# A query-bias product for four pairs at once: stationary and moving sides exchanged in a cross-attention kernel

## The chip, the core and the metric

The kernel runs on one core of a Trainium2 chip. The metric is the device time of one execution in microseconds (us), the median over several runs. The engines are TensorE (PE in the profile, with its weight loads as PEld), VectorE (DVE), ScalarE (ACT), GpSimd (POOL) and SyncE (SP, which here only issues DMAs). SBUF is the core's working memory, PSUM the memory with eight banks that TensorE writes to.

## The reference, cut to what matters

The program is one block of a Perceiver: cross-attention of 64 queries over 1601 context rows, for a batch of 8; then an attention among the 64 queries with 16 heads; then a layer of eight experts of which each token takes one. All is float32. The change touches the cross-attention alone:

```python
qp = layernorm(x) @ Wq + bq            # (8, 64, 512)
kp = ctx @ Wk + bk                     # (8, 1601, 512)
vp = ctx @ Wv + bv
attn = softmax((qp @ kp.T) / sqrt(512))
x = x + attn @ vp
```

The kernel never forms kp. It uses qp·kp = (qp·Wkᵀ)·ctx + qp·bk. The second term is one number per query, called q.bk or `qb` here. It is added to every score of its row.

## The kernel before

The 8 x 64 = 512 tokens are handled as four pairs of batch entries, 128 tokens each (`NT` = 4, `P` = 128). Channels (512) are four chunks of 128 (`DC` = 4). The helper names below are those of the code.

**The start.** x is normalised with tokens on partitions and transposed on TensorE (`turn_x`, L271), so that channels lie on partitions (`xnT`). `project_q` (L279) multiplies by Wq and writes `qpT`: query channels on partitions, tokens along the free side. It runs once for pair 0 (L298) and once for pairs 1 to 3 together (L835). ScalarE adds bq while it copies from PSUM (L289).

**Two products of each pair's queries.** `keyed(p)` (L308) computes qp·Wkᵀ, with tokens on partitions; ScalarE copies it to a row `qk` (L313). `biased(p)` (L315) computes q.bk: the pair's queries are the stationary side, a 128x128 block for each of four chunks, and one column of `bk` is the moving side. The result, one column with tokens on partitions, is copied by ScalarE to column p of `qb` (L324). The softmax needs it in that form: one number per partition, read by VectorE in L375 and L377.

**The scores.** `spread(p)` (L326, GpSimd) repeats each run of 32 channels of qk four times, and `fill_queries` (L345) transposes these on TensorE into the tile `R` (L349; ScalarE copies at L352). The context comes by DMA with rows on partitions. VectorE turns it into blocks of 32 by 32 (`blocks`, L245, with L233 and L240), four of whose parts make a tile `T`; five buffers (pool `blk`) hold the T tiles, and the softmax's `L` tiles too. `scores` (L354) multiplies T by R for a quarter of the channels, in tiles of 32 rows by 64 columns of the array, into four PSUM banks. `softmax` (L367) follows on VectorE and ScalarE, `chances` (L400) transposes the result, and `attend` (L409) multiplies by the context.

**Order.** TensorE's order is written out by hand from L252 on (a manual schedule); that of ScalarE is too in the block at L829. Elsewhere the tile framework orders each engine's instructions by its own planning, from their place in the program and their dependencies. So a line moved in the program moves exactly on TensorE, and about so on VectorE and ScalarE.

**The loop.** From L851, for each pair p, four quarters of scores with earlier stages of pair p-2 among them, the softmax, then preparation of the next pair, then `attend` in four groups. In pair 0 the preparation has `keyed` and `biased` for pairs 1 to 3 one after the other (L879 to L883), then `tables` (L629), whose product is `gs` (L639).

**Buffers.** Big tiles (weights, context, `xnT`, `qpT`) are slabs, of which there are 12. The loads of pair 1's context and of the next weights wait in SP's queue until a slab comes free: the one of `wkT` after the last `keyed`, that of `qpT` after its last reader, those of the context after `attend`. PSUM tiles take whole banks, eight in all.

Of the kernel before, what the change touches and what calls it, by code (L numbers as in the profile page):

```python
# [10 lines left out]
F32 = mybir.dt.float32  # L11
# [6 lines left out]
P = 128  # L18
B, S, D = 8, 64, 512
SK = 1601  # L20
NT = B * S // P
DC = D // P
# [14 lines left out]
def perceiver_kernel(ctx: ExitStack, tc: tile.TileContext, out: bass.AP, t: dict):  # L37
    nc = tc.nc
# [6 lines left out]
    rowp = pool(name="rows", bufs=22)  # L45
# [5 lines left out]
    def slab(name):  # L51
        return slabs.tile([P, DC, D], F32, tag="slab", name=name)

    def row(name):
        return rowp.tile([P, D], F32, tag="row", name=name)
# [4 lines left out]
    def bank(name):  # L60
        return banks.tile([P, D], F32, tag="bank", name=name)

    def bank4(name):
        return banks.tile([P, DC, P], F32, tag="bank", name=name)
# [25 lines left out]
    ident = const.tile([P, P], F32, tag="ident", name="ident")  # L90
    make_identity(nc, ident)

    def load_c(name, shape, queue):
        c = const.tile(shape, F32, tag=name, name=f"c_{name}")
        return c, queue.dma_start(out=c, in_=t[name])

    def load_late(name, shape):
        c, ins = load_c(name, shape, nc.gpsimd)
        tc.keep_in_program_order(ins)
        return c  # L100

    def load_b(name, n, c=None):
        if c is None:
            c = const.tile([P, n], F32, tag=name, name=f"c_{name}")
        tc.keep_in_program_order(
            nc.gpsimd.dma_start(out=c, in_=t[name].partition_broadcast(P))
        )
        return c

    bq, _ = load_c("xbq", [P, DC], nc.scalar)  # L110
    bk, _ = load_c("xbk", [P, DC], nc.scalar)
# [22 lines left out]
    qb = const.tile([P, NT], F32, tag="qb", name="qb")  # L134
# [110 lines left out]
    def blocks(p, q, b2):  # L245

        T = block_tile(p, q, b2)
        for g in range(4):
            turn_group(T, p, q, b2, g)
        return T  # L250
# [4 lines left out]
    qpT = slab("qpT")  # L255
# [15 lines left out]
    def turn_x(i, xn):  # L271
        tp = transposed(xn, f"xn{i}")
        step = 2 if i == 0 else DC
        for dc in range(0, DC, step):
            nc.scalar.copy(  # L275
                xnT[:, dc : dc + step, i * P : (i + 1) * P], tp[:, dc : dc + step, :]
            )
# [30 lines left out]
    def keyed(p):  # L308

        cols = slice(p * P, (p + 1) * P)  # L310
        ps = projected(qpT[:, :, cols], wkT, f"qk{p}")
        qks[p] = row(f"qk{p}")
        nc.scalar.copy(qks[p], ps)  # L313

    def biased(p):  # L315

        cols = slice(p * P, (p + 1) * P)
        ps = bank(f"qb{p}")
        for ec in range(DC):
            nc.tensor.matmul(  # L320
                ps[:, 0:1], lhsT=qpT[:, ec, cols],
                rhs=bk[:, ec : ec + 1], start=(ec == 0), stop=(ec == DC - 1),
            )
        nc.scalar.copy(qb[:, p : p + 1], ps[:, 0:1])  # L324

    def spread(p):  # L326

        qk = qks.pop(p)
        got = []
        for b0 in range(0, NB, 4):  # L330
            q4 = rowp.tile([P, 4, 4, 32], F32, tag="row", name=f"q4_{p}_{b0}")
            nc.gpsimd.tensor_copy(  # L332
                q4,
                qk[:, 32 * b0 : 32 * b0 + 128].rearrange(
                    "p (b d) -> p b d", d=32
                ).unsqueeze(2).to_broadcast([P, 4, 4, 32]),
            )
            got.append(q4)
        return got

    def queries(p):

        return one.tile([P, NB, P], F32, tag="R", name=f"R_{p}")

    def fill_queries(p, R, q4s, half):  # L345
        for b0 in range(8 * half, 8 * half + 8, 4):
            tp = bank4(f"rt_{p}_{b0}")
            for j in range(4):
                nc.tensor.transpose(  # L349
                    tp[:, j, :], q4s[b0 // 4][:, j, :, :].rearrange("p a d -> p (a d)"), ident  # L350
                )
            nc.scalar.copy(R[:, b0 : b0 + 4, :], tp)  # L352

    def scores(p, q, R, sc, Ts, js=range(4)):  # L354
        for j in js:
            b = 4 * q + j
            for a in range(4):
                for b2 in range(2):
                    r = b2 * S
                    nc.tensor.matmul(  # L360
                        sc[a][r : r + S, : WIDTH[a]],
                        lhsT=R[32 * a : 32 * a + 32, b, r : r + S],
                        rhs=Ts[b2][32 * a : 32 * a + 32, j, : WIDTH[a]],
                        start=(b == 0), stop=(b == NB - 1),
                    )
# [456 lines left out]
    def quarter(p, q):  # L822
        return [blocks(p, q, b2) for b2 in range(2)]

    def do(*steps):
        for f, i in steps:
            f(i)

    with tc.manual_schedule(engines={mybir.EngineType.Activation}):  # L829
        keyed(0)  # L830
        for i in range(1, NT):
            turn_x(i, later[i - 1])
        biased(0)
    q4s = spread(0)
    project_q(1, NT - 1, [bank(f"qp1_{ec}") for ec in range(DC)])  # L835
    R = queries(0)
    fill_queries(0, R, q4s, 0)
    fill_queries(0, R, q4s, 1)
    bv = load_b("xbv", D, row("c_xbv"))
    lnw = load_late("lnw", [P, DC])  # L840
    lnb = load_late("lnb", [P, DC])
# [9 lines left out]
    for p in range(NT):  # L851
        i = p - 2
        if 0 < p < NT - 1:
            q4s = spread(p + 1)
        sc = [bank(f"sc_{p}_{a}") for a in range(4)]
        for q in range(4):
            if p == 0 and q == 0:
                nTs = [first[1, 0], first[1, 1]]
            elif p == 0 and q == 1:
                nTs = [first[2, 0], blocks(0, 2, 1)]  # L860
            else:
                nTs = quarter(p, q + 1) if q < 3 else None
            if i >= 0 and q == 3:
                scores(p, q, R, sc, Ts, range(3))
                do((back, i))
                scores(p, q, R, sc, Ts, (3,))
            else:
                scores(p, q, R, sc, Ts)
            Ts = nTs
            if i >= 0 and q < 3:  # L870
                do(((split, align, sums)[q], i))
        L, r = softmax(p, sc)
        pts = []

        def chance():
            pts.append(chances(p, len(pts), L))

        if p == 0:
            for k in range(1, NT):  # L879
                keyed(k)  # L880
                biased(k)
                if k == 1:
                    q4s = spread(1)  # L883
            tables()
        else:
            do((at_turn, p - 1))
            if i >= 0:
                do((output, i))
        if p + 1 < NT:
            R = queries(p + 1)  # L890
            if p == 0:
                chance()
                fill_queries(1, R, q4s, 0)
            elif p == 1:
                fill_queries(2, R, q4s, 0)
                do((at_out, 0))
                chance()
            else:
                do((at_out, p - 1))
                fill_queries(p + 1, R, q4s, 0)  # L900
                chance()
            fill_queries(p + 1, R, q4s, 1)
        else:
            at_out(p - 1, chance)
        if 0 < p < NT - 1:
            load_pair(p + 1)
        if p == 1:
            blank_rows()
        ac = bank(f"ac_{p}")
        if i >= 0:  # L910
            do((face, i))
        for g in range(4):
            if g < 3:
                chance()
            if p > 0 and g == 3:
                do((turn, p - 1))
            attend(p, g, pts[g], ac)
            if p > 0 and g == 0:
                do((norm, p - 1))
            if i >= 0 and g == 0:  # L920
                do((gated, i))
            if i >= 0 and g == 1:
                do((routed, i))
        tile_of[p]["acs"] = divided(p, ac, r)
        if 0 < p < NT - 1:
            do((unit_q, p - 1))
            Ts = quarter(p + 1, 0)
            do((unit_k, p - 1), (gates, p - 1), (values, p - 1))
        elif p == 0:
            Ts = quarter(1, 0)  # L930
# [92 lines left out]
    ps = bank("pc")  # L1023
# [14 lines left out]
    with tc.If(spill != 0), ExitStack() as ph:  # L1038
# [4 lines left out]
        for i in range(NT):  # L1043
            x3 = row(f"dx3_{i}")
            layernorm(x3, xs[i], f"d{i}")
            tp = ps_g.tile([P, DC, P], F32, tag="gu", name=f"dxt{i}")
# [8 lines left out]
        for e in range(E):  # L1055
# [11 lines left out]
                wb, lhsT=ones, rhs=dg.rearrange("p i q -> p (i q)"), start=True, stop=True  # L1067
# [6 lines left out]
            for ic in range(IC):  # L1074
                pgu = []
                for k in range(2):
                    ps = ps_g.tile([P, B * S], F32, tag="gu", name=f"dgu{e}_{ic}_{k}")
                    for dc in range(DC):
                        c0 = k * FI + ic * P
                        nc.tensor.matmul(  # L1080
                            ps, lhsT=wgu[:, dc, c0 : c0 + P], rhs=xsT[:, dc, :],
                            start=(dc == 0), stop=(dc == DC - 1),
# [6 lines left out]
            for i in range(NT):  # L1089
                for ic in range(IC):  # L1090
                    nc.tensor.matmul(
                        acc[i], lhsT=h[:, ic, i * P : (i + 1) * P], rhs=wd[:, ic, :],
                        start=(e == 0 and ic == 0), stop=(e == E - 1 and ic == IC - 1),
# [58 lines left out]
```

## Time and profile before

| What | Value |
|---|---|
| Median of 3 runs | 303.27 us (302.66 to 303.32) |
| Profiled execution, device time | 302.67 us |
| Its span, first to last instruction | 300.9 us |
| Mean granted TensorE clock | 0.995 of full |
| qb products (L320), passes and busy time | 32, 3.8 us |
| qb copies (L324) | 4, 0.159 us median |
| Mean DMA rate over the span | 192 GB/s |

The profile is of one execution. Its rows group instructions by line, engine, operation and the program's names, with the shape of the tile written and read. A float32 product appears as two passes, so four products of one `biased` are eight matmul rows. A matmul's end is modelled, and successive ones overlap in the records: for the cost of a group take the distance from its start to the start of the next, not the length of its rows. The waits name the engine, what it waited for, the total, the number of times and the longest. A share of busy time is an average over very different stages: the first 45 us, where data is still coming in, and the rest.

### The profile page before, as it was taken

To read this page: it belongs to the slowest core of one execution; us is meant where nothing else is said; L and a number is where in the kernel's file an instruction comes from. 1 tells how busy PE (TensorE), PEld (TensorE's weight loads), DVE (VectorE), ACT (ScalarE), POOL (GpSimd) and SP (SyncE) were. 2 spreads that over 40 slices of the span, in tenths; PEclk is the share of its full clock that TensorE was granted. 3 is DMA by queue.
4 is the path that set the end of the run, shared out by engine and by line. 5 is a ranking of instruction groups with operands and counts; after the bars stand their busy time and mean duration, and the time that the engine had idled before them with its cause. 6 is when DMAs were issued, how large, how long until landed. Compare 5 with 4: busy or idle time off the path is not lost. (4 is left out here: it accounts for less than half of the span.)

```text
span 300.9 us, 6426 instructions
## 1 busy us (share of the span) xinstructions
PE 287.7 (96%) x2652; PEld 149.0 (50%) x2652; DVE 161.7 (54%) x412; ACT 91.8 (31%) x198; POOL 61.0 (20%) x93
## 2 busy tenths in 40 slices
PE   6999899999999999999999999999999999899991
PEld 5866655743554344656434475443454557343320
DVE  2465469135743487956568785552472475364230
ACT  2223205330037021417704134632426324121110
POOL 4065200500081004200220300032050032203301
PEclk9999999999999999999999999999999999999997
DMA  6999960279984993000299102969990200603601
GB/s 187 350 417 396 345 271 1 54 296 395 397 291 151 347 418 105 3 2 0 85 408 367 51 4 67 344 190 353 370 353 4 72 0 2 210 34 94 190 2 43
DMA packets 20288, 57.71 MB, mean 192 GB/s; under 512 B 2274, under 2 KB 10514, under 8 KB 16544
## 3 DMA queue, kind: packets, MB, share of 16 engines
q1 hardware_dynamic: 17568, 50.37, 46.8%
q0 software_dynamic: 2400, 6.89, 6.2%
q8 instruction: 23, 0.38, 0.5%
q14 instruction: 9, 0.07, 0.1%
q10 hardware_dynamic: 288, 0.00, 0.1%
HBM read 50.94 MB, written 6.84 MB: 192 GB/s over the span
## 5 line engine op out<-in xcount | busy, mean ns | idle before, releaser
L233 DVE STREAM_TRANSPOSE T<-cx 128x512 f32<-128x512 f32 x96 | 61.8, 680 | 25.0 <-DMA cx<-in_ctx_dram 18.6
L360 PE MATMUL sc<-T,R 32*64 32x416 f32 (+2 forms) x1024 | 49.5, 501 | 1.5 <-DVE T L233 1.0
L416 PE MATMUL ac<-cx,pt 128*64 128x512 f32 x192 | 43.8, 598 | 0.0
L360 PEld LDWEIGHTS sc<-T,R 32*64 32x64 f32 x1024 | 26.6, 131 | 19.1 <-issue 7.1
L416 PEld LDWEIGHTS ac<-cx,pt 128*64 128x64 f32 x192 | 12.7, 136 | 22.4 <-issue 21.6
L960 PE MATMUL gu<-wgu,xeT 128*32 128x512 f32 x192 | 23.0, 597 | 0.0
L492 POOL TENSOR_TENSOR gm_k<-qn_k,c_gk 128x512 f32<-128x512 f32 x4 | 5.1, 1272 | 62.5 <-DVE qn_k L487 42.8
L455 POOL TENSOR_TENSOR x<-x,c_bo 128x512 f32<-128x512 f32 x4 | 5.1, 1268 | 59.5 <-DVE xh L454 59.5
L284 PE MATMUL qp<-xnT,w_xWq 128*128 128x128 f32 (+1 forms) x64 | 16.2, 424 | 0.5 <-ACT xnT L275 0.5
L332 POOL COPY q<-qk 128x512 f32<-128x512 f32 x16 | 9.0, 611 | 34.3 <-ACT qb L324 21.3
L185 PE MATMUL p_qk<-w_xWkT,qpT 128*128 128x512 f32 x32 | 15.0, 605 | 0.0
L185 PE MATMUL p_q<-w_aWq,xhT 128*128 128x512 f32 x32 | 14.8, 605 | 0.0
L185 PE MATMUL p_k<-w_aWk,xhT 128*128 128x512 f32 x32 | 14.7, 595 | 0.0
L185 PE MATMUL p_po<-w_xWv,acT 128*128 128x512 f32 x32 | 14.7, 595 | 0.0
L185 PE MATMUL p_o<-w_aWo,cT 128*128 128x512 f32 x32 | 14.5, 596 | 0.0
L406 ACT COPY pt<-pp 128x512 f32<-128x512 f32 (+1 forms) x16 | 8.3, 516 | 20.4 <-PE pp L404 20.2
L185 PE MATMUL p_v<-w_aWv,xvT 128*128 128x512 f32 x32 | 14.4, 592 | 0.0
L284 PEld LDWEIGHTS qp<-xnT,w_xWq 128*128 128x128 f32 x64 | 11.5, 230 | 5.0 <-ACT xnT L275 0.9
L371 DVE TENSOR_REDUCE mx<-sc 128x1 f32<-128x416 f32 (+2 forms) x16 | 8.1, 567 | 10.8 <-PE sc L360 10.8
L995 PE MATMUL y<-wd,hT 128*32 128x512 f32 x96 | 11.5, 596 | 0.6 <-DVE hT L987 0.6
L960 PEld LDWEIGHTS gu<-wgu,xeT 128*32 128x32 f32 x192 | 6.0, 109 | 8.9 <-issue 8.2
L185 PEld LDWEIGHTS p_q<-w_aWq,xhT 128*128 128x128 f32 x32 | 5.7, 189 | 9.0 <-issue 5.9
(189 smaller groups left out, 398.8 us busy)
## 6 DMA issues: line engine op xcount, KB each, us to landing
cx<-in_ctx_dram SPq DMA_DIRECT2D x24, 1024.0 KB, 9.9
wgu<-in_wgT_dram SPq DMA_DIRECT2D x8, 512.0 KB, 9.3
wgu<-in_wuT_dram SPq DMA_DIRECT2D x8, 512.0 KB, 10.0
wd<-in_wdT_dram SPq DMA_DIRECT2D x8, 512.0 KB, 9.6
rd<-blank POOLq DMA_DIRECT2D x6, 258.0 KB, 5.0
in<-rd SPq DMA_DIRECT2D x6, 258.0 KB, 4.2
xd<-blank POOLq DMA_DIRECT2D x6, 256.0 KB, 4.3
in<-xd SPq DMA_DIRECT2D x6, 256.0 KB, 7.2
```

The source lines that it names most:

```text
L185: nc.tensor.matmul(ps, lhsT=srcT[:, dc, :], rhs=w[:, dc, :], start=(dc == 0), stop=(dc == DC - 1),)
L233: nc.vector.transpose(T[:, :, 128 * g : 128 * g + 128].rearrange("p b (c k) -> p b c k", k=32), cxs[p, g][b2][:, :, 128 * q : 128 * q + 12 ...
L284: nc.tensor.matmul(ps[ec][:, : n * P], lhsT=wq[:, dc, ec * P : (ec + 1) * P], rhs=xnT[:, dc, cols], start=(dc == 0), stop=(dc == DC - 1),)
L332: nc.gpsimd.tensor_copy(q4, qk[:, 32 * b0 : 32 * b0 + 128].rearrange("p (b d) -> p b d", d=32).unsqueeze(2).to_broadcast([P, 4, 4, 32]),)
L360: nc.tensor.matmul(sc[a][r : r + S, : WIDTH[a]], lhsT=R[32 * a : 32 * a + 32, b, r : r + S], rhs=Ts[b2][32 * a : 32 * a + 32, j, : WIDTH[a ...
L371: nc.vector.tensor_reduce(mx[:, a : a + 1], sc[a][:, : WIDTH[a]], AX.X, ALU.max)
L406: nc.scalar.copy(pt[:m, :nch, :], tp[:m, :nch, :])
L416: nc.tensor.matmul(ac[r : r + S, :], lhsT=pt[:m, j, r : r + S], rhs=rhs, start=(g == 0 and j == 0), stop=(g == 3),)
L455: nc.gpsimd.tensor_tensor(xs[i], xs[i], bo, ALU.add)
L492: nc.gpsimd.tensor_tensor(heads(gm), heads(qn), gb.unsqueeze(1).to_broadcast([P, H, HD]), ALU.mult)
L960: nc.tensor.matmul(ps[c, :], lhsT=xTs[k][:, dc, c], rhs=ffw[e][0][:, dc, :], start=(dc == 0), stop=(dc == DC - 1),)
L995: nc.tensor.matmul(y[c, :], lhsT=hT[:, ic, c], rhs=ffw[e][1][:, ic, :], start=(ic == 0), stop=(ic == IC - 1),)
```

## The change

The four calls of `biased(p)` become one `biased()`. It runs after all queries are there: after the transposes that fill `R` for pair 0, before the first scores. Now `bk` is the stationary side: for each chunk, one column is read 32 times over (a broadcast), which makes a 128x32 block. The queries of a pair move, 128 tokens at a time. The four pairs write to four groups of 32 partitions of one PSUM bank, so that pair p uses the array's p-th group of 32 columns. Each of the 32 partitions of a group then holds the same row: q.bk for 128 tokens along the free side. ScalarE copies the 128x128 block to SBUF.

A new `unturned` brings tokens to partitions: one 128x128 transpose on TensorE, issued behind the first quarter of pair 0's scores, and a VectorE copy of every 32nd column from PSUM into `qb` (128x4). The readers of `qb` are unchanged.

```diff
-    def biased(p):
-
-        cols = slice(p * P, (p + 1) * P)
-        ps = bank(f"qb{p}")
+    def biased():
+
+        ps = bank("qb")
         for ec in range(DC):
-            nc.tensor.matmul(
-                ps[:, 0:1], lhsT=qpT[:, ec, cols],
-                rhs=bk[:, ec : ec + 1], start=(ec == 0), stop=(ec == DC - 1),
-            )
-        nc.scalar.copy(qb[:, p : p + 1], ps[:, 0:1])
+            for p in range(NT):
+                nc.tensor.matmul(
+                    ps[32 * p : 32 * p + 32, :P],
+                    lhsT=bk[:, ec : ec + 1].to_broadcast([P, 32]),
+                    rhs=qpT[:, ec, p * P : (p + 1) * P],
+                    start=(ec == 0), stop=(ec == DC - 1),
+                )
+        qbT = rowp.tile([P, P], F32, tag="row", name="qbT")
+        nc.scalar.copy(qbT, ps[:, :P])
+        return qbT
+
+    def unturned(qbT):
+        tp = bank4("t_qb")
+        nc.tensor.transpose(tp[:, 0, :], qbT, ident)
+        nc.vector.tensor_copy(qb, tp[:, 0, ::32])
...
             turn_x(i, later[i - 1])
-        biased(0)
     q4s = spread(0)
     project_q(1, NT - 1, [bank(f"qp1_{ec}") for ec in range(DC)])
     R = queries(0)
     fill_queries(0, R, q4s, 0)
     fill_queries(0, R, q4s, 1)
+    qbT = biased()
...
             else:
                 scores(p, q, R, sc, Ts)
             Ts = nTs
+            if p == 0 and q == 0:
+                unturned(qbT)
...
             for k in range(1, NT):
                 keyed(k)
-                biased(k)
                 if k == 1:
                     q4s = spread(1)
```

## The prediction

> **What bounds the kernel now.** I read the page first, for the engines' shares and the clock; then TensorE's waits over the whole span; then its timeline from the start to 62 us, with VectorE's and ScalarE's beside it; and last the same engines where pair 1 starts.
>
> ```profile
> span 300.9 us, 6426 instructions
> PE 287.7 (96%) x2652; PEld 149.0 (50%) x2652; DVE 161.7 (54%) x412; ACT 91.8 (31%) x198; POOL 61.0 (20%) x93
> ```
>
> TensorE is busy for 96% of the span (its ends are modelled, so this alone proves little). Its list of waits is the stronger evidence:
>
> ```profile
> PE idle L118 <- POOL ident masks.py:199: 2.0, 1, 2.0
> PE t_c L177 <- DVE cg L552: 1.6, 2, 1.1
> PE sc L360 <- DVE T L233: 1.0, 1, 1.0
> PE y L995 <- DVE hT L987: 0.6, 1, 0.6
> PE sc L360 <- DVE T L240: 0.6, 1, 0.6
> ```
>
> Between 45 and 237 us only one wait is listed, 0.3 us at 91.16. So a microsecond of TensorE work there is a microsecond of the span, if its feeders keep up. Before 45 us it does wait, and there its work is cheap. The changed products stand on both sides of that border, in TensorE's timeline:
>
> ```profile
> 17.89 0.95 PE L320 MATMUL qb<-c_xbk,qpT 128*128 128x1 f32 x8
> 18.89 10.59 PE L284 MATMUL qp<-xnT,w_xWq 128*128 128x384 f32 x32
> 29.31 1.91 PE L349 MATMUL rt<-ident,q 128*128 128x128 f32 x16
> 31.15 0.91 PE L360 MATMUL sc<-T,R 32*64 32x416 f32 x2
> 33.03 8.64 PE L360 MATMUL sc<-T,R 32*64 32x416 f32 x192 [0.97 <-DVE T L233]
> 42.24 3.02 PE L360 MATMUL sc<-T,R 32*64 32x416 f32 x62 [0.57 <-DVE T L240]
> 45.19 3.70 PE L185 MATMUL p_qk<-w_xWkT,qpT 128*128 128x512 f32 x8
> 48.72 0.95 PE L320 MATMUL qb<-c_xbk,qpT 128*128 128x1 f32 x8
> 49.53 3.68 PE L185 MATMUL p_qk<-w_xWkT,qpT 128*128 128x512 f32 x8
> 53.05 0.95 PE L320 MATMUL qb<-c_xbk,qpT 128*128 128x1 f32 x8
> 53.86 3.68 PE L185 MATMUL p_qk<-w_xWkT,qpT 128*128 128x512 f32 x8
> 57.38 0.95 PE L320 MATMUL qb<-c_xbk,qpT 128*128 128x1 f32 x8
> 58.19 0.39 PE L639 MATMUL gs<-c_gwT,ones 128*128 128x32 f32 x2
> ```
>
> Columns: start, length, engine, line, what, count. Each float32 product stands as two passes (four products, x8). The first qb fills a wait; the other three stand between products that follow without a gap. VectorE and ScalarE at the same places:
>
> ```profile
> 17.26 1.57 ACT L275 COPY xnT<-t_xn 128x512 f32<-128x512 f32 x3
> 32.27 1.30 DVE L233 STREAM_TRANSPOSE T<-cx 128x512 f32<-128x512 f32 x2 [1.28 <-DMA cx<-in_ctx_dram]
> 36.16 1.90 DVE L233 STREAM_TRANSPOSE T<-cx 128x512 f32<-128x512 f32 x3 [2.58 <-PE sc L360]
> 41.92 0.26 DVE L240 STREAM_TRANSPOSE T<-tail 96x128 f32<-96x128 f32 x1
> ```
>
> So pair 0's scores are set by VectorE: the first quarter waits until 33.03 for a tile that a DMA holds back; its end frees the buffer for three more tiles (36.16 to 42.18, no gap); the last quarter waits for these at 42.24.
>
> [...]little is saved by one column: eight passes at 128x1 take 0.81 us start to start, 0.10 each, while a 128x128 transpose takes 0.11 (8 in 0.88 at 140.46). [...]four transposes between scores take 0.59 (131.65 to 132.24) against 0.44 for four amid other transposes, 0.15 for in and out. [...]the experts' 128*32 products at 512 columns issue four in 0.43 us (weight loads at 228.01 and 228.44), which is what one 512-column pass takes alone (p_k's eight in 3.43).
>
> **The change, part by part.**
> 1. Removed behind 45 us: three qb blocks. Start to start: 49.53-48.72, 53.86-53.05 and 58.19-57.38, 0.81 each, 2.43. A p_qk behind another should also take 3.43, as p_k does (109.79 to 113.22), instead of the 3.52 seen beside qb: up to 0.18 more. I take -2.5 (-2.4 to -2.6). No cover hides these. What is late next, with TensorE 2.5 earlier: gs and the first transposes of L would run at 55.7 and 56.0; L's exponentials end at 52.4. The 16 transposes for R need GpSimd's copies of qk1, issued from 53.04 at 0.6 each, four by 55.3; they would be asked for from about 56.4. Both are in time by 1 us or more.
> 2. Removed at 17.89: the block of pair 0. The product behind it starts at 18.89, right after ScalarE's last xnT copy ends (17.26+1.57=18.83). Worth 0; TensorE waits there instead. The four tiny ScalarE copies (0.16 each) stand where ScalarE has idle time: 0.
> 3. Added behind the 16 transposes at about 31.2: 16 products, 32 passes of 128*32 by 128 columns, as eight rounds of four column groups. A round costs at least 128/512 of 0.43, 0.107; if the weight load (0.109 for 32 columns on the page) isn't hidden, 0.22. That is 0.9 to 1.8 us, with 0.2 to 0.3 for mode changes 1.1 to 2.0; I take 1.3. The queries are all there (ScalarE's L289 ends at 30.1). Behind them on TensorE stands the first score, which can't pass 33.03 anyway: 1.8 us of cover from 31.2. So 0, at worst +0.2; without the cover it would be +1.3, as it would also push the start of VectorE at 36.16. If the groups do not overlap it is much more (rival 3).
> 4. Added: a 128x128 ScalarE copy at about 32.5. ScalarE's R copies end at 32.03 and it then idles for 16.5 us: 0.
> 5. Added after the first quarter of scores (about 35.9): one transpose between scores, 0.11+0.15=0.26 on TensorE. The quarters behind it end at 41.7+0.26=41.9, still before 42.24, where the last waits for VectorE. Hidden: 0.
> 6. Added on VectorE: a copy of 128x4 from PSUM, in the very stretch (36.16 to 42.18) that ends the wait at 42.24. Nearest row: the 128x8 reduction L644, 0.19. If it stands among the tiles it costs 0.2 in full; if the compiler puts it ahead of them, VectorE waits for the transpose too (0.3 to 0.4) and it costs 0.6; behind them it is free. What waits behind it is the tiles, and for these the scores. I take +0.2 (0 to +0.6).
> 7. SP's queue: loads at 57.57 wait for the slabs of wkT and qpT, which the last p_qk now frees about 1.5 us earlier (57.4 to about 55.8), so pair 1's context starts earlier too. They move by 1.5 where TensorE moves by 2.3. Pair 1's scores start at 73.61 and VectorE's last tile before them ends at 72.55: 1.06 of slack, minus up to 0.8. Just enough: 0, at worst +0.5. Later loads are issued when TensorE's attention products free slabs, so they move with it. GpSimd's queue gets nothing.
>
> Sum: -2.5+0.2=-2.3 for the span. The profiled execution took 302.67, which gives 300.4. It is 0.6 below the median of the runs shown (303.27; the three lie at 302.66, 303.27 and 303.32), from which it would be 301.0. I say 300.7, between them.
>
> **The rivals.**
> 1. VectorE's stretch takes more back: the copy leads the tiles (0.6 instead of 0.2), and the new products outlast their cover a little (+0.2). For it: the stretch has no gap at all. Against: a tile is ready before the copy is. -2.5+0.8=-1.7: 301.3.
> 2. The gain is swallowed where pair 1 starts: its context tiles, or an order on VectorE or ScalarE that comes out otherwise, hold the scores at about 73. For it: the DMA engines are 73 to 101% busy from 58 to 74 us, and the slack is 1.06. Against: the loads themselves are released by TensorE. If 0.8 to 1.8 is lost: -1.5 to -0.5, say 301.9.
> 3. Slower: the column groups do not overlap when the stationary side is one column repeated 32 times, and each pass runs alone. Price: the 128-column passes of the first query product take 5.66/32=0.177 each; 32 make 5.7 us, from 31.2 to 36.9. Past the cover of 1.8 this delays the first quarter, then VectorE at 36.16, by 3.9. -2.3+3.9=+1.6: 304.6. It decides from about 4.1 us for the block (1.8 of cover and 2.3 of gain), 0.13 a pass. Against: the experts' products overlap; for: no row has a repeated stationary column.
> 4. The change does less than it says: the removed blocks were hidden. Only the one at 17.89 is; at the other three no wait is recorded.
>
> **How the numbers follow.** Forecast (300.7) 0.62; rival 1 0.14; rival 2 0.10; rival 3 or another late feeder of its size 0.14. A change of 0.2%, 0.6 us, is about what a measurement of this kernel can tell from none. The forecast, rival 1 and most of rival 2 are faster: 0.82; the rest of rival 2 and the edge of rival 3 are the same: 0.06; slower: 0.12. The range: from the best ends (-2.6 on the profiled execution, 300.1) down to 300.0, and up through rivals 1 and 2 to 302.4, where 0.14 is left above and little below.
>
> **What would show it.** Right: p_qk blocks of 3.43 to 3.5 us back to back, gs at about 55.9; the new block under 1.8 us and the scores starting at 33.0; VectorE's three tiles ending at 42.2 to 42.4; pair 1's scores at about 71.3 without a wait. Wrong: a block of 4 us or more, a score start past 33.2, a new wait of TensorE near 70, or a copy that makes VectorE idle at 36.

## The result, and the profile after

The changed kernel takes 300.77 us in the median of 20 runs (299.83 to 303.34), the kernel before 303.22 of 20 (302.02 to 306.54). The ratio is 0.9912, with a 95% interval of 0.9887 to 0.9937: 2.7 us faster, between 1.9 and 3.4 (the two medians differ by 2.45). Runs more than 1.5% above the fastest of their kernel count as slow and are left out of every ratio, and of the medians quoted below.

The page after, its span and engines:

```profile
span 298.4 us, 6424 instructions
PE 283.8 (95%) x2653; PEld 144.1 (48%) x2653; DVE 162.3 (54%) x413; ACT 91.6 (31%) x195; POOL 61.0 (20%) x93
```

The span is 2.5 us shorter and TensorE's busy time 3.9. The second figure is no measure of the change: 2.0 us of it are two waits for a weight DMA between 10 and 15 us in this execution, ahead of every changed line. A later profile of the same kernel, `after_again`, has 285.5 us of busy time.

TensorE's timeline of the kernel after, over the changed places (start, length, engine, line, what, count):

```profile
18.64 10.59 PE L284 MATMUL qp<-xnT,w_xWq 128*128 128x384 f32 x32 [0.83 <-ACT xnT L275]
29.06 1.91 PE L358 MATMUL rt<-ident,q 128*128 128x128 f32 x16
30.90 1.08 PE L320 MATMUL qb<-qpT,c_xbk 128*32 128x128 f32 x32
31.91 0.91 PE L369 MATMUL sc<-T,R 32*64 32x416 f32 x2
33.12 3.02 PE L369 MATMUL sc<-T,R 32*64 32x416 f32 x62 [0.30 <-DVE T L233]
36.07 0.33 PE L332 MATMUL t_qb<-ident,qbT 128*128 128x128 f32 x1
36.33 9.09 PE L369 MATMUL sc<-T,R 32*64 32x416 f32 x192
45.35 10.57 PE L185 MATMUL p_qk<-w_xWkT,qpT 128*128 128x512 f32 x24
55.75 0.30 PE L648 MATMUL gs<-c_gwT,ones 128*128 128x32 f32 x2
55.89 0.63 PE L413 MATMUL pp<-ident,L 128*128 128x128 f32 x4
```

The old block at 17.9 has become a wait of 0.83, and the product behind it starts where ScalarE lets it, as before. The new block takes 1.01 us start to start (30.90 to 31.91), and behind it TensorE still waits for VectorE's tile until 33.12. The three p_qk are one row: 10.40 us from 45.35 to 55.75, where p_qk (the product of `keyed`) and qb by turns took 13.00 (45.19 to 58.19).

VectorE over pair 0's scores, of the same kernel:

```profile
32.36 1.31 DVE L233 STREAM_TRANSPOSE T<-cx 128x512 f32<-128x512 f32 x2 [1.14 <-DMA cx<-in_ctx_dram]
36.25 0.71 DVE L233 STREAM_TRANSPOSE T<-cx 128x512 f32<-128x512 f32 x1 [2.58 <-PE sc L369]
36.88 0.12 DVE L333 COPY qb<-t_qb 128x4 f32<-128x4 f32 x1
42.08 0.26 DVE L240 STREAM_TRANSPOSE T<-tail 96x128 f32<-96x128 f32 x1
```

The copy stands behind the first tile and waits for nothing. From the first tile's start to the last one's end it is 6.09 us, against 6.02 before: it costs 0.07.

**A measure with little noise.** The start of these kernels varies from run to run, by when DMAs land: VectorE's two last tiles, released by a DMA in every kernel here, start between 31.55 and 32.79 in these profiles. TensorE's first transpose of pair 0's L (`pp`, at 58.41 before) is where all kernels are alike again. The time between them, D, was 58.41-32.27=26.14 before and 55.89-32.36=23.53 after. The changed kernel was run twice more beside others: 55.80-32.27 and 55.08-31.55, both 23.53. So the change is worth 2.61 in this stretch. From there to the end it takes 242.5 in both first profiles (300.9-58.41 and 298.4-55.89), so nothing of the gain is given back later. Four kernels profiled beside each other on one chip bear this out: with D between 23.53 and 28.17 they all take 241.2 to 241.4 for the rest (`after_again`, `old_form_new_place`, `new_form_old_place`, `block_three_times`).

D has one limit. Where the work ahead of the scores outlasts the wait for the tile, D also holds how long before its tile TensorE reached that work, and this varies from run to run: 1.2 us in `after_beside` (31.55-30.32), 1.7 in `block_three_times` (32.11-30.39). For such versions a few tenths of D mean nothing.

### The profile page after: what moved, and what is told of

Same layout as the page of the kernel before. It is cut to its first block, busy times and chain, and to the rows that moved or that the text cites. A ratio compares the mean times of both kernels' runs of the same rounds, so it can differ in the third digit from the quotient of the medians.

```text
span 298.4 us, 6424 instructions
## 1 busy us (share of the span) xinstructions
PE 283.8 (95%) x2653; PEld 144.1 (48%) x2653; DVE 162.3 (54%) x413; ACT 91.6 (31%) x195; POOL 61.0 (20%) x93
## 5 line engine op out<-in xcount | busy, mean ns | idle before, releaser
L284 PE MATMUL qp<-xnT,w_xWq 128*128 128x128 f32 (+1 forms) x64 | 14.4, 384 | 1.3 <-ACT xnT L275 1.3
L284 PEld LDWEIGHTS qp<-xnT,w_xWq 128*128 128x128 f32 x64 | 9.6, 191 | 5.7 <-ACT xnT L275 1.8
L185 PEld LDWEIGHTS p_qk<-w_xWkT,qpT 128*128 128x128 f32 x32 | 5.8, 190 | 9.9 <-issue 8.3
```

The lines of the kernel that those rows point to most:

```text
L185: nc.tensor.matmul(ps, lhsT=srcT[:, dc, :], rhs=w[:, dc, :], start=(dc == 0), stop=(dc == DC - 1),)
L284: nc.tensor.matmul(ps[ec][:, : n * P], lhsT=wq[:, dc, ec * P : (ec + 1) * P], rhs=xnT[:, dc, cols], start=(dc == 0), stop=(dc == DC - 1),)
```

## Experiments

D and the ratio to the kernel before, measured beside each, with its 95% interval, for all runs:

| Run | D, us | D against before | Ratio of the times |
|---|---|---|---|
| before | 26.14 | | 1 |
| changed kernel | 23.53 | -2.61 | 0.9912 [0.9887, 0.9937] |
| after_again | 23.53 | -2.61 | 0.9907 [0.9877, 0.9936] |
| old_form_new_place | 28.17 | +2.03 | 0.9982 [0.9956, 1.0007] |
| old_form_look (one run) | 28.24 | +2.10 | |
| old_form_wide | 24.84 | -1.30 | 0.9940 [0.9917, 0.9963] |
| new_form_old_place | 24.67 | -1.47 | 0.9929 [0.9905, 0.9952] |
| block_three_times | 23.83 | -2.31 | 0.9912 [0.9883, 0.9942] |
| one_group | 25.02 | -1.12 | 0.9948 [0.9928, 0.9968] |
| key_half_early | 22.68 | -3.46 | 0.9863 [0.9823, 0.9903] |
| after_beside | 23.53 | -2.61 | 0.9871 [0.9826, 0.9915] |
| key_one_early | 22.69 | -3.45 | 0.9863 [0.9824, 0.9902] |
| key_half_beside | 22.69 | -3.45 | 0.9874 [0.9832, 0.9917] |
| scalar_copy | 23.46 | -2.68 | 0.9871 [0.9831, 0.9912] |

The theory: a gain where TensorE is the bound (45 us on), bought with work laid under a wait of TensorE (31 to 33 us). Rivals: only the amount of TensorE's work counts, wherever it stands; or only the place does.

### Form and place apart

The change does two things, a move and another form. Two kernels do one each; the changed kernel was measured beside them (`after_again`).

> The changed kernel itself, as the measure for the runs beside it. Expected from its first measurement: 2.5 us (0.8%) below the kernel before, with the product gs about 2.4 us earlier in the trace than before (55.75 against 58.19).

The move alone, against the kernel before:

```diff
         for i in range(1, NT):
             turn_x(i, later[i - 1])
-        biased(0)
...
     fill_queries(0, R, q4s, 1)
+    for k in range(NT):
+        biased(k)
...
                 keyed(k)
-                biased(k)
```

> All four pairs' products in the old form (queries stationary, one column of bk moving, no transpose), moved to the new place ahead of pair 0's scores. Theory (cover): four blocks of 0.81 take 3.2 us from about 31.0, the scores can't start before 33.1 anyway, so they start about 1.3 late, at 34.4; the three p_qk still close up by 2.6. Net 1.2 to 1.3 us faster than before. Rival (TensorE's total decides, not the place): the same products as before, so no gain, 0 within 0.3. Rival (the place alone, all of it is hidden there): 2.5 us faster.

Measured: 0.9982, at most 1.3 us faster, where 1.2 to 1.3 was expected; and its profile is worse than that, D up by 2.03. TensorE's timeline there:

```profile
30.70 4.62 PE L320 MATMUL qb<-c_xbk,qpT 128*128 128x1 f32 x32
35.25 14.55 PE L360 MATMUL sc<-T,R 32*64 32x416 f32 x256
49.73 10.57 PE L185 MATMUL p_qk<-w_xWkT,qpT 128*128 128x512 f32 x24
```

Four old blocks should take 3.2 (four times 0.81); they took 4.55, and the scores 14.48 (49.73-35.25). The view by windows says why. Its columns are the window, its length, the busy time of the five engines with counts, then the granted TensorE clock, the DMA share and GB/s:

```profile
32.00:33.00 1.00, 1.00 (x11) 1.00 (x11) 0.89 (x2) 0.16 (x1) 0.00 (x0) 1.00 1.07 375
33.00:34.00 1.00, 1.00 (x7) 1.00 (x7) 0.41 (x1) 0.16 (x1) 0.00 (x0) 0.56 1.11 225
34.00:35.00 1.00, 1.00 (x7) 1.00 (x6) 0.00 (x0) 0.00 (x0) 0.00 (x0) 0.50 0.93 256
39.00:40.00 1.00, 1.00 (x20) 0.67 (x14) 0.00 (x0) 0.00 (x0) 0.00 (x0) 0.53 1.06 442
40.00:41.00 1.00, 1.00 (x36) 0.79 (x28) 0.30 (x1) 0.00 (x0) 0.00 (x0) 1.00 0.95 393
```

The clock was halved, from about 33.1 to 39.9, though TensorE counts as busy all through. No theory had this; it is taken up below. This run alone therefore doesn't separate form from place.

The form alone: pair 0 keeps its old block at 17.9, and the new block stands behind the last p_qk, where nothing hides it. Against the changed kernel:

```diff
             turn_x(i, later[i - 1])
+        biased_one(0)
...
-    qbT = biased()
...
-            if p == 0 and q == 0:
-                unturned(qbT)
...
                 if k == 1:
                     q4s = spread(1)
+            qbT = biased()
             tables()
...
             fill_queries(p + 1, R, q4s, 1)
+            if p == 0:
+                unturned(qbT)
```

(`biased_one` is the old `biased`.)

> The new form (column groups, one transpose), but behind the last p_qk of pair 0, where the old blocks stood; pair 0 keeps its old block at 17.9, and the transpose stands among the other transposes at about 58. Theory (cover): there nothing hides the new block, so its 1.0 us, 0.1 to 0.2 of mode change and 0.1 of transpose stand in full against the 2.4 to 2.6 removed: 1.2 to 1.4 us faster than before, so that gs begins at about 56.9. Rival (TensorE's total decides): 2.5 us faster less the old block of pair 0 that is kept, at least 2 us. Rival (the place alone): 0.

```profile
44.94 10.57 PE L185 MATMUL p_qk<-w_xWkT,qpT 128*128 128x512 f32 x24
55.44 1.08 PE L331 MATMUL qb<-qpT,c_xbk 128*32 128x128 f32 x32
56.45 0.41 PE L659 MATMUL gs<-c_gwT,ones 128*128 128x32 f32 x2
56.69 0.64 PE L424 MATMUL pp<-ident,L 128*128 128x128 f32 x4
```

The block costs its 1.01 here in full (55.44 to 56.45). D is down by 1.47, and the transpose behind it costs 0.11 more (58.91 to 59.02): 1.36, as the theory of cover had it. In time it is 2.1 faster (1.5 to 2.9), which leans to the rival's figure; but against the changed kernel beside it the medians differ by only 0.54 (300.34 and 299.80), with intervals that overlap, while D puts 1.14 between them. The time can't tell 1.3 from 2.1 here; the trace can.

### The price of the block and the size of its cover

```diff
-        for ec in range(DC):
+        for ec in 3 * list(range(DC)):
```

> The changed kernel with the new block of 32 passes run three times over, with the same result. It adds 64 passes, 1.7 to 2.0 us, from about 31.8. Theory (cover): the wait still open behind the block, about 1.1 us (31.91 to 33.12, less the two score passes in it), swallows part; the scores start 0.7 to 1.0 late and the end moves by as much: about 1.6 us faster than before in place of 2.5. Rival (no cover, work is work): 0.5 to 0.8 faster than before. Rival (column groups stop overlapping when there are more of them): slower than before.

```profile
30.39 2.83 PE L320 MATMUL qb<-qpT,c_xbk 128*32 128x128 f32 x96
33.15 3.02 PE L369 MATMUL sc<-T,R 32*64 32x416 f32 x64
```

96 passes take 2.76 us; the 64 added ones 1.75, so 0.109 for a round of four. One 128-column pass alone would need 0.107 by an estimate, a quarter of the 0.43 of a 512-column pass. So the four column groups run fully side by side, also with one stationary column repeated. D rises by 0.30 for 1.75 of added work: nearly all is hidden. I had expected 0.7 to 1.0. The wait had been measured in the first profile, less a tenth for the two score passes in it. In this run TensorE came to the block 0.51 earlier than there (30.39 against 30.90) and the tile only 0.25 earlier (32.11 against 32.36), so the room was larger by a quarter of a microsecond. The rival without cover (0.5 to 0.8 faster than before) is out.

The same product without column groups:

```diff
-            for p in range(NT):
-                nc.tensor.matmul(
-                    ps[32 * p : 32 * p + 32, :P],
-                    lhsT=bk[:, ec : ec + 1].to_broadcast([P, 32]),
-                    rhs=qpT[:, ec, p * P : (p + 1) * P],
...
+            nc.tensor.matmul(
+                ps[:32, :],
+                lhsT=bk[:, ec : ec + 1].to_broadcast([P, 32]),
+                rhs=qpT[:, ec, :],
...
-        qbT = rowp.tile([P, P], F32, tag="row", name="qbT")
-        nc.scalar.copy(qbT, ps[:, :P])
+        qbT = row("qbT")
+        nc.scalar.copy(qbT[:32, :], ps[:32, :])
...
-        nc.tensor.transpose(tp[:, 0, :], qbT, ident)
-        nc.vector.tensor_copy(qb, tp[:, 0, ::32])
+        for p in range(NT):
+            nc.tensor.transpose(tp[:, p, :32], qbT[:32, p * P : (p + 1) * P], ident[:32, :32])
+        nc.vector.tensor_copy(qb, tp[:, :, 0])
```

> The new form without column groups: bk stationary, all 512 tokens moved at once into the first group of 32 columns, four products in place of 16, and four small transposes in place of one. Theory (groups run together): the array now takes 8 passes of 512 columns one after another, 8 x 0.43 = 3.4 us in place of 1.0, from about 30.7 to 34.2; the scores start about 1.1 late and three more transposes cost 0.3 or less: 1.1 to 1.4 us faster than before in place of 2.5 to 3. Rival (the groups did not matter): as fast as the changed kernel.

```profile
31.48 3.62 PE L319 MATMUL qb<-qpT,c_xbk 128*32 128x512 f32 x8
35.03 3.02 PE L369 MATMUL sc<-T,R 32*64 32x416 f32 x64
```

The block takes 3.55, and the scores start at 35.03, 1.6 after their tile is there (VectorE's row at 32.79 plus 0.67). D is down by 1.12, the time by 1.6 (1.0 to 2.2). So the groups are worth 2.5 us of TensorE and 1.5 of the end: the rest of the slower block disappears in the wait.

### Why the clock fell

> A second look at the kernel with the old form at the new place, in whose first trace TensorE's granted clock fell to half from about 33.1 to 39.9 us. Theory (clock): [...]the fall comes again[...], with scores that start near 35 and end near 49.7. Rival (a chance event of that run): a clock of 1.00 there, scores from 34.0 to about 46.2 us, and a span near 298.5.

A second execution shows the same fall:

```profile
33.00:34.00 1.00, 1.00 (x8) 1.00 (x7) 0.28 (x1) 0.16 (x1) 0.00 (x0) 0.60 1.03 236
36.00:38.00 2.00, 2.00 (x36) 1.03 (x32) 0.00 (x0) 0.00 (x0) 0.00 (x0) 0.50 0.94 360
40.00:42.00 2.00, 2.00 (x56) 1.37 (x45) 1.35 (x3) 0.00 (x0) 0.00 (x0) 0.99 0.90 369
```

The single column may be the cause, or the place, or the weight loads. So the same stationary blocks at the same place, with a moving side that is wide:

```diff
-                ps[:, 0:1], lhsT=qpT[:, ec, cols],
-                rhs=bk[:, ec : ec + 1], start=(ec == 0), stop=(ec == DC - 1),
+                ps[:, :P], lhsT=qpT[:, ec, cols],
+                rhs=bk[:, ec : ec + 1].to_broadcast([P, P]), start=(ec == 0), stop=(ec == DC - 1),
```

> The old form at the new place, with the column of bk read 128 times over as the moving side: the same stationary blocks and weight loads, 128 equal columns out in place of one. Theory (clock): the block is as long as before in time (32 passes at 0.10 to 0.11, 3.2 to 3.5 us), [...]the clock stays at 1.00; the block ends at 34.0 to 34.3 and costs only what outlasts the cover, about 1 us: 1.4 to 1.7 us faster than the kernel before. Rival (the place or the weight loads make the clock fall): the clock falls again and the time is that of the first old form, 0.5 us faster than before or less.

```profile
33.00:34.00 1.00, 1.00 (x11) 1.00 (x10) 1.00 (x2) 0.16 (x1) 0.00 (x0) 1.00 1.13 256
36.00:38.00 2.00, 2.00 (x60) 1.49 (x50) 0.00 (x0) 0.00 (x0) 0.00 (x0) 1.00 1.00 363
```

```profile
31.22 3.74 PE L320 MATMUL qb<-c_xbk,qpT 128*128 128x128 f32 x32
34.88 12.24 PE L360 MATMUL sc<-T,R 32*64 32x416 f32 x256
47.05 10.57 PE L185 MATMUL p_qk<-w_xWkT,qpT 128*128 128x512 f32 x24
```

The clock stays at 1.00, the block takes 3.66 (31.22 to 34.88), a little more than expected, and the scores 12.17 (34.88 to 47.05). Moving 128 columns in place of one makes the end earlier: D is 3.3 us smaller. It is neither the place nor the weight loads, then, but the width of the moving side. This is also the test of the move without the fall of the clock: 1.30 by D, just under the 1.4 to 1.7 expected, and 1.8 by the time (1.1 to 2.5). Move (1.30) and form (1.36) are each worth about half, and together 2.61. Beside the old form as it was, with its single column, the new form is worth more at the new place: it also spares the fall.

One thing stays open. The time of old_form_new_place is better than its two profiles say (+2.0 by D, but -0.5 us with an interval that ends at +0.2). The mean granted clock of each run is on record, and it suggests why. The two profiled executions have 0.985 and 0.983; half the clock for 6.8 of some 300 us is a loss of 1.1%, by my estimate. Of the other runs two more lie at 0.985 or 0.986; with the first profiled one these three take 303.2 us in the mean. Seven lie at 0.989 or 0.990, about what, by the same estimate, a fall of half that length would leave, and take 301.9; three at 0.992 or above take 301.5. All runs of old_form_wide lie at 0.991 or above. So the fall seems to be shorter or absent in most executions. This isn't shown: those runs left no trace, and runs of the kernel before spread from 0.985 to 0.998 too, though only 12 of 47 lie at 0.990 or below.

### Using the rest of the wait

Some wait is left behind the new block. Part of pair 1's p_qk fits there: the first one or two of its four products, the others where they were.

```diff
     qbT = biased()
+    keyed_part(1, range(1))
...
-                keyed(k)
+                if k == 1:
+                    keyed_part(1, range(1, DC))
+                else:
+                    keyed(k)
```

(`keyed_part` issues those of the chunks that it is given, into one bank that stays taken until the last; `range(2)` moves two.)

> The changed kernel, with the first half of pair 1's product with the key weights (two of four products, 4 passes of 512 columns, 1.72 us) moved from behind the scores into the wait that is still open behind the new block. The three-fold block showed that about 1.75 us fits there with at most 0.1 to 0.2 of delay. Theory (cover): scores start 0.2 to 0.5 later, p_qk is 1.7 shorter, 1.2 to 1.5 us faster than the changed kernel, so 4 us below the kernel before. Rival (what follows 45 us is not set by TensorE alone: L's exponentials or pair 1's context tiles are late next): less than 0.5 us.

> The changed kernel, as the measure beside the next three: 2.4 to 3.0 us (0.8 to 1.0%) below the kernel before.

> One of the four products of pair 1's p_qk (2 passes, 0.86 us with up to 0.1 of mode change) moved into the wait behind the new block, which was 1.13 us long behind a block that ended at 31.99. Theory (cover): it fits whole, the scores start where they did, and p_qk is 0.86 shorter: 0.7 to 0.9 us faster than the changed kernel beside it. Rival (the cover is used up by the new block): no faster.

> Two of the four products moved, beside the changed kernel on one chip. Its first trace had the scores 0.78 late and p_qk 1.72 shorter: 0.9 to 1.0 us faster than the changed kernel. If this holds, the second product brings no more than 0.2 over the first, since what outlasts the cover is paid again.

```profile
30.84 1.08 PE L336 MATMUL qb<-qpT,c_xbk 128*32 128x128 f32 x32
31.85 1.12 PE L323 MATMUL qk<-w_xWkT,qpT 128*128 128x512 f32 x2
32.91 3.02 PE L385 MATMUL sc<-T,R 32*64 32x416 f32 x64
45.15 2.84 PE L323 MATMUL qk<-w_xWkT,qpT 128*128 128x512 f32 x6
```

This is key_one_early. The product fits the wait whole: the scores start 0.76 behind the start of their tile (32.91-32.15), as in the changed kernel (33.12-32.36), and D is 0.84 below the changed kernel's, as expected. Two products give 0.85 (twice): the second outlasts the cover by what it saves. The first forecast for two, 1.2 to 1.5, missed. It took the room from block_three_times, where TensorE reached the place 1.72 us before the tile; in key_half_early it was 1.31 (32.29-30.98). The time doesn't resolve these versions: 300.0 and 299.96 beside 300.2, with intervals of 0.4% each way. (The changed kernel itself came out at 0.9871 on this chip, better than the 0.8 to 1.0% expected, at the same D as always.) And a part is lost again late: the expert input that TensorE transposes at about 220 us comes by a DMA, and TensorE waits for it 0.49 and 0.71 in these two against 0.25 in the changed kernel beside them. From the end of D to the end of the span they take 243.2 and 243.4 against 242.7. key_half_early, on another chip, has no such wait.

```profile
219.62 0.63 PE L177 MATMUL t_xe<-ident,in 128*128 128x128 f32 x4 [0.49 <-DMA in<-xd]
```

So by D key_one_early is as good as any version, but about half of its 0.84 is gone by the end of the span, and what is left is less than its time can show.

### The small copy

```diff
-        nc.vector.tensor_copy(qb, tp[:, 0, ::32])
+        nc.scalar.copy(qb, tp[:, 0, ::32])
```

> The changed kernel with the copy of 128x4 into qb on ScalarE, which is idle there, in place of VectorE. Theory (VectorE's run of tiles sets the end of pair 0's scores): the tiles end 0.05 to 0.1 earlier counted from the start of the first, and the last scores by as much; in the time no more than 0.1, not to be told from no change. Rival (the copy costs the 0.2 of the prediction, or more): 0.2 us faster or better, with the last tile 6.0 us after the first starts in place of 6.1 and more.

VectorE's tiles take 6.03 (36.36 to 42.39) in place of 6.09, and D falls by 0.07; the time shows nothing (0.9871 for both). The copy costs 0.07, not 0.2.

## Why the prediction was right

The predicted time was 300.7, the measured 300.77; that the two agree so closely is chance, for the terms were off by some tenths. By its steps:

1. *The three blocks, -2.5 (-2.4 to -2.6).* From the first p_qk to the first `pp`: 58.41-45.19=13.22 before, 55.89-45.35=10.54 after, so -2.68. The p_qk do close up, to 3.47 each; and gs to pp shrank by a further 0.08, which the range left out. What was named as late next was not late: L's last exponential ended at 52.2, and GpSimd's eight copies began at 52.71, at 0.56 each in time for 56.36.
2. *The block at 17.9, 0.* Right: a wait of 0.83 stands there, ended by ScalarE's xnT, and every other run without that block shows the same.
3. *The new block, 1.3 with mode changes, hidden by 1.8.* It took 1.01, a little below the range of 1.1 to 2.0: eight rounds at 0.109 are 0.87, and only 0.14 is left for the mode changes, that is, for going from 128*128 tiles to 128*32 and on to 32*64, for which 0.2 to 0.3 was added. The cover was put at 1.8; in the three profiles of the changed kernel it was 2.0 to 2.4 (33.12-30.90=2.2 in the first), since it depends on when the tile's DMA lands: the tile starts between 31.55 and 32.36 there. That the weight load of 0.105 to 0.110 is hidden, for which both ends were kept, is shown by the 0.109 of a round, which has four passes and four loads.
4. *ScalarE's copy, 0.* Right: at 32.05, 0.27 behind the R copies, in ScalarE's idle time.
5. *The transpose among the scores, 0.26, hidden.* It took 0.26 (36.07 to 36.33). The 0.57 of wait at 42.24 is gone from TensorE's list, and its weight loads still wait for the last tile at 42.40.
6. *The copy on VectorE, +0.2 (0 to +0.6).* Too dear: 0.07. The copy itself took 0.12, against the 0.19 of its nearest row, and the run of tiles around it became only 0.07 longer. Placed behind the first tile, it had nothing to wait for.
7. *SP's queue, 0 (at worst +0.5).* The loads were issued at 55.94 in place of 57.57, 1.6 earlier. VectorE's last tile before pair 1's scores ended 1.06 before they started, exactly as before (69.76+0.27 and 71.09): that run of tiles is released by TensorE's own transposes of L (VectorE waits 0.84 for `pp` before it, 1.61 in the kernel before), not by the load, so the slack lost nothing.

The sum of -2.3 was -2.61 in D, -2.5 in the span. Rival 1 asked for the copy ahead of the tiles and the block past its cover: neither came. Rival 2, a loss at pair 1: none. Rival 3 asked for 0.13 a pass or more; it was 0.03 (1.01 for 32). Its price of 0.177 for a pass alone was too high. It was read from a row of the first query product that was drawn out, for a reason that stays open: 6 or 7 passes a microsecond from 8 to 11 us, 11 in the next. The same 32 passes take 3.84 in the changed kernel's profile (from 6.72 us), 0.12 each, and the 32 of old_form_wide take 3.66. So even one after another the passes would, by an estimate from these two, have stayed under the 4.1 us at which the rival decides; one_group, without the groups, took 3.55 and was faster than the kernel before. Rival 4 is refuted by the first step.

## What to carry to other kernels

Before work on the busiest engine is cut, find on its timeline which of it stands in a wait and which in an unbroken row: of four equal blocks here one was worth nothing and three their full 0.8 each. Work that must stay is best put under a wait of the same engine that a DMA sets, and this wait is measured by adding work until the end moves. Its room differs from run to run (2.0 to 2.4 us in the changed kernel), so leave some tenths of it free. To compare versions that differ by less than the noise of a run, take the distance between an event that a DMA sets and one behind the change; this is exact only while the engine still waits for that event.

## What the runs showed of the hardware

Here a row of products that move a single column each let TensorE's clock fall, though the engine counts as busy the whole time. In two profiles of 32 such passes the granted clock went to 0.50 about 2.4 and 2.6 us after the first of them (33.1 and 33.2, from 30.70 and 30.64) and stayed there for 6.8 us. With 128 equal columns moved, all else the same, it stayed at 1.00 (one profile, old_form_wide). The eight-pass blocks of the kernel before (0.81 each, among wide products) show no such fall: the clock is 1.00 at all of them. What sets the onset of the fall and its length the runs do not show.

Four column groups of 32, with 128 float32 columns moved, cost 0.109 us a round of four passes, weight loads included, about the 0.107 estimated for one such pass by its columns alone, from the 0.43 of a 512-column pass. Without the groups, 512 columns in each pass took 0.44 (3.55 for eight, one_group).
